# The fourth layer's experts in three passes instead of two, and a finer turn order around them

## The chip, the cores and the metric

The kernel runs on one core of a Trainium2 chip. The metric is device time in microseconds for one execution; a kernel's time is the median of several runs. TensorE is called PE here, VectorE DVE, ScalarE ACT, GpSimd POOL and SyncE SP. SP does no arithmetic in this kernel; it issues nearly all DMAs, in its program's order.

## The reference, cut to what matters

Eight layers follow each other on `x` of 8 batches of 512 rows of 128 numbers, in fp32. Each is added to `x` behind two layer norms:

```python
x = x + _layernorm(_L0_attn_ref(_layernorm(x), ...))   # softmax attention
x = x + _layernorm(_L0_ffn_ref(_layernorm(x), ...))    # token mix, gated
x = x + _layernorm(_L1_attn_ref(_layernorm(x), ...))   # a small network, trained step by step
x = x + _layernorm(_L1_ffn_ref(_layernorm(x), ...))    # 8 experts, one per row
x = x + _layernorm(_L2_attn_ref(_layernorm(x), ...))   # linear attention
x = x + _layernorm(_L2_ffn_ref(_layernorm(x), ...))    # 8 experts, each picks its rows
x = x + _layernorm(_L3_attn_ref(_layernorm(x), ...))   # softmax attention
x = x + _layernorm(_L3_ffn_ref(_layernorm(x), ...))    # 4 experts by position
```

The third layer is a scan over the 8 batches: each step computes gradients of a two-layer network (with an exact gelu, so an error function), updates its weights, and uses the new weights for its output; batch 7 has to wait for batch 6. The fourth layer sends each row to one expert, with a place counted from the first batch on, and drops rows beyond an expert's 256 places:

```python
oh = (routes[:, None] == jnp.arange(E)[None, :]).astype(jnp.int32)
pos = (jnp.cumsum(oh, axis=0) * oh).sum(-1) - 1
keep = pos < capacity
slot = jnp.where(keep, routes * capacity + pos, E * capacity)
buf = jnp.zeros((E * capacity + 1, D), x.dtype).at[slot].set(x)
h = jax.nn.relu(jnp.einsum('ecd,edh->ech', buf_e, w1) + b1[:, None, :])
y = jnp.einsum('ech,ehd->ecd', h, w2) + b2[:, None, :]
out = jnp.where(keep[:, None], y_flat[slot], x)
```

The sixth layer's experts each choose the best 512 of all 4096 rows, so it can't begin before every batch has left the fifth.

## The kernel before, in words

The program is written in the order in which Python generators are stepped, and each engine executes its instructions in that order. There are four stages.

The first stage is the first attention (`Attention.run` inside `l0`). It steps generators of the second to fourth layers between its own matmuls: `Mix.chain` (second layer), `Learn.chain` and `Learn.serve_chain` (third layer: the weight updates, and the outputs), and `Route.chain` (fourth layer: which expert and which place; it ends with four scatters, L1060, that write a batch's rows into a table by expert). These generators are still running when the attention's own work is at its end, and are handed on. Before its first load the attention calls `Route.clear` (L966), which writes zeros into the tables by expert with DMAs on SP's queue.

The second stage is called "between", and is where the change is made. An object `Rounds` holds the list of generators; `turn` steps each of them once, in the order of the list. To the generators that came from the first stage two are added:

- `Passes.chain` computes the fourth layer's experts. `PASSES = (5, B)` says that one pass serves batches 0 to 4 and another batches 5 to 7. A pass (`once`) runs all eight experts over the whole table of 8 x 256 places, whatever has been filled. It waits until its batches are routed (`while route.done < n: yield`). For an expert it loads rows (L1130), transposes them (L1136), and computes `l1f_h_ps` (L1148) with relu on ACT and DVE (L1159, L1161), then `l1f_y_ps` (L1170), adds the bias (L1172) and writes the result. Its weights, 512 KB an expert, are loaded three experts ahead. One turn holds one piece of three experts: `taken(e)`, `given(e - 2)`, `hidden(e - 1)`.
- `Pairs.chain` starts the fifth layer, one generator (`batch`) for each batch: gather the experts' results (L1265), norm, add, norm, `qkv` (L1304), linear attention, add, and the preparation of the sixth layer, whose last instruction is the store of `l2f_x` (L1406). A batch can start when its pass is done, and 5 turns after the batch ahead of it. The first one also waits for the second layer's end (`mix.over`), because the table of ACT functions is changed then. A batch has 29 steps; most are one operation on one engine, then a `yield`.

In this stage `cx.brisk` is set, so every `yield from cx.soft(...)` is no yield: the third layer's error function (L810 to L829) is one piece of DVE instructions there.

When the last batch has been routed (`while route.done < B`), the tiles of the first chains are released and `Experts` (sixth layer) loads its first weights, in the midst of the stage; `raw_b` and the transposes of L179 belong to it. The stage ends when no generator is left.

The third stage is the sixth layer, which begins with a search for each expert's threshold (from L1491 on). The fourth stage is the last attention with the last layer between its matmuls.

Tiles come from pools with a given number of buffers, in turn: `l2_o` has 3, `l2_xT` 2, the table of `qkv` tiles 4. All PSUM tiles share a ring of eight banks (`Ctx.bank`).

Of the kernel before, what the change touches and what calls it, by code (L numbers as in the profile page):

```python
# [18 lines left out]
B = 8  # L19
# [26 lines left out]

CAP1 = T // NE // 2

PASSES = (5, B)
FAR = 1 << 16  # L50


# [190 lines left out]
def free(pe=0.0, dve=0.0):  # L243

    return pe, dve, True
# [15 lines left out]
class Background:  # L261
# [19 lines left out]
    def step(self, queue, gen):  # L281
        try:
            pe, dve, is_free = costs(next(gen))
        except StopIteration:
            queue.remove(gen)
            return
        self.pe += pe
        self.dve += dve
        (self.free.add if is_free else self.free.discard)(gen)

    def turn(self, gen):

        self.first.remove(gen)
        self.first.append(gen)
        self.step(self.first, gen)
# [397 lines left out]
class Learn:  # L693
# [75 lines left out]
    def step(self, b, last):  # L769
        cx, nc = self.cx, self.cx.nc  # L770
# [39 lines left out]
        nc.vector.tensor_scalar(c, a, 0.7071067811865476, 4.0, ALU.mult, ALU.min)  # L810
        nc.vector.tensor_scalar_max(c, c, -4.0)
        nc.vector.tensor_mul(x2, c, c)
        yield from cx.soft(free(0.0, 0.9))
        nc.vector.tensor_scalar_mul(p, x2, ERF_A[0])
        for v in ERF_A[1:-1]:
            nc.vector.scalar_tensor_tensor(p, p, v, x2, ALU.add, ALU.mult)
        nc.vector.scalar_tensor_tensor(p, p, ERF_A[-1], c, ALU.add, ALU.mult)
        yield from cx.soft(free(0.0, 2.3))
        nc.vector.tensor_scalar_mul(q, x2, ERF_B[0])
        for v in ERF_B[1:-1]:  # L820
            nc.vector.scalar_tensor_tensor(q, q, v, x2, ALU.add, ALU.mult)
        nc.vector.tensor_scalar_add(q, q, ERF_B[-1])
        yield from cx.soft(free(0.0, 1.4))
        nc.vector.reciprocal(q, q)
        yield from cx.soft(free(0.0, 1.7))
        nc.vector.tensor_mul(p, p, q)
        phi, h = tile_of("phi"), tile_of("h", 2)
        nc.vector.tensor_scalar(phi, p, 0.5, 0.5, ALU.mult, ALU.add)
# [106 lines left out]
class Route:  # L935
# [5 lines left out]
    def __init__(self, cx: Ctx, w_switch, b_switch):  # L941
# [8 lines left out]
            cx.dram.tile([NE * CAP1, D], F32, name=f"l1f_{name}{i}", tag=f"l1f_{name}{i}")  # L950
            for i in range(len(PASSES))
        ]
# [24 lines left out]
    def turn(self, b):  # L977
        return sum(b >= n for n in PASSES)

# [102 lines left out]
class Passes:  # L1082
# [14 lines left out]
    def weights(self, n):  # L1097

        cx, nc, e = self.cx, self.cx.nc, n % NE
        if n >= len(PASSES) * NE:  # L1100
            return
# [18 lines left out]
    def once(self, base, rows, results):  # L1120
        cx, nc = self.cx, self.cx.nc
        NF = self.NF
        cap, ns = CAP1, CAP1 // P
        of_expert = lambda t, e: t[e * cap : (e + 1) * cap, :].rearrange("(s p) d -> p s d", p=P)
        loads, xts, hts = {}, {}, {}

        def load(e):
            if e < NE:
                loads[e] = cx.work([P, ns, D], "l1f_xg", bufs=4)
                nc.sync.dma_start(loads[e], of_expert(rows, e))  # L1130

        def taken(e):
            xg = loads.pop(e)
            t = cx.bank("l1f_xT_ps")
            for s in range(ns):
                nc.tensor.transpose(t[:, s * P : (s + 1) * P], xg[:, s, :], cx.ident)  # L1136
            xts[e] = cx.work([D, cap], "l1f_xT")
            nc.vector.tensor_copy(xts[e], t[:, :cap])
            load(e + 4)

        def hidden(e):
            hts[e] = cx.work([P, NF, cap], "l1f_hT")
            xt = xts.pop(e)
            for f2 in range(NF // 2):
                hp = cx.bank("l1f_h_ps")
                for i in range(2):
                    f = 2 * f2 + i
                    nc.tensor.matmul(  # L1148
                        hp[:, i * cap : (i + 1) * cap],
                        self.ws[base + e][0][:, f * P : (f + 1) * P],  # L1150
                        xt,
                        start=True,
                        stop=True,
                    )
                for i in range(2):
                    f = 2 * f2 + i
                    src, bias = hp[:, i * cap : (i + 1) * cap], self.b1c[:, f, e : e + 1]
                    if i == 0:
                        nc.scalar.activation(hts[e][:, f, :], src, AF.Relu, bias=bias)  # L1159
                    else:  # L1160
                        nc.vector.tensor_scalar(hts[e][:, f, :], src, bias, 0.0, ALU.add, ALU.max)  # L1161

        def given(e):
            ht = hts.pop(e)
            w2 = self.ws.pop(base + e)[1]
            yp = cx.bank("l1f_y_ps")
            for s in range(ns):
                ss = slice(s * P, (s + 1) * P)
                for f in range(NF):
                    nc.tensor.matmul(yp[:, ss], ht[:, f, ss], w2[:, f, :], start=(f == 0), stop=(f == NF - 1))  # L1170
            y = cx.work([P, ns, D], "l1f_y")
            nc.vector.tensor_add(  # L1172
                y,
                yp[:, :cap].rearrange("p (s d) -> p s d", d=D),
                self.b2b[:, e * D : (e + 1) * D].unsqueeze(1).to_broadcast([P, ns, D]),
            )
            nc.sync.dma_start(of_expert(results, e), y)
            self.weights(base + e + 3)

        for e in range(4):  # L1180
            load(e)
        yield
        for e in range(NE + 2):
            if e < NE:
                taken(e)
            if e >= 2:
                given(e - 2)
            if 1 <= e <= NE:
                hidden(e - 1)
            yield  # L1190


class Rounds:


    def __init__(self, chains):
        self.chains = list(chains)

    def add(self, chain):
        self.chains.append(chain)  # L1200

    def turn(self):
        for chain in list(self.chains):
            try:
                next(chain)
            except StopIteration:
                self.chains.remove(chain)


class Pairs:  # L1210
# [23 lines left out]
    def chain(self, passes, mix, rounds):  # L1234

        cx = self.cx
        for _ in range(3):
            yield
        self.w, self.gw = (
            cx.transposed(w, n, raw=raw) for w, n, raw in zip(self.args, ("w2a", "w2f_gate"), self.raws)  # L1240
        )
        while not mix.over:
            yield
        cx.nc.scalar.preload_act_table_set("natural_log_exp_and_others")
        for b in range(B):
            while passes.done <= self.route.turn(b):
                yield
            rounds.add(self.batch(b))
            for _ in range(5 if b + 1 < B else 0):
                yield  # L1250

    def batch(self, b):
        cx, nc, route = self.cx, self.cx.nc, self.route
# [696 lines left out]
@with_exitstack  # L1950
def kernel(ctx: ExitStack, tc: tile.TileContext, a: dict, out: bass.AP):
    cx = Ctx(ctx, tc, a["consts"])
    nc = tc.nc
    for b in range(B):
        nc.sync.dma_start(cx.x[b], a["L0_attn_x"][b].rearrange("(j p) d -> p j d", p=P))
    of = lambda layer, *names: [a[f"{layer}_{n}"] for n in names]
    route = Route(cx, *of("L1_ffn", "w_switch", "b_switch"))
    right = ExitStack()
    with cx.phase("first"):
        cx.w = right.enter_context(tc.tile_pool(name="chains", bufs=2, side="right"))  # L1960
        with cx.beside("attention") as ca:
            mix = Mix(cx, *of("L0_ffn", "W_r", "W_k", "W_v", "mu_r", "mu_k"))
            learn = Learn(cx, route, *of("L1_attn", "t_k", "t_v", "t_q", "W1", "b1", "W2", "b2"))
            chains = l0(cx, Attention(ca), *of("L0_attn", "Wq", "Wk", "Wv"), mix, learn)

        cx.brisk = True
        with cx.beside("between") as cb:
            rounds = Rounds(chains)
            passes = Passes(cb, route, *of("L1_ffn", "w1", "b1", "w2", "b2"))
            pairs = Pairs(cb, route, *of("L2_attn", "W_qkv"), *of("L2_ffn", "gate_w"))  # L1970
            rounds.add(passes.chain())
            rounds.add(pairs.chain(passes, mix, rounds))
            while route.done < B:
                rounds.turn()
            right.close()
            ce = right.enter_context(cx.beside("experts", side="right"))
            experts = Experts(ce, pairs, *of("L2_ffn", "ln_w", "ln_b", "fc1s", "b1s", "fc2s", "b2s"))
            while rounds.chains:
                rounds.turn()
    cx.brisk = False  # L1980
    with cx.phase("last"):
        at = Attention(cx)
        ffn = L3Ffn(cx, *of("L3_ffn", "W1", "b1", "W2", "b2", "Wu", "bu"), out)
        with cx.beside("staging") as cs:
            cs.home = cx.home
            weights = l3_weights(cs, *of("L3_attn", "Wqkv", "bqkv", "Wout", "bout"))
            ffn.load()
            weights = experts.run(cs, weights)
        right.close()
        cx.w = right.enter_context(tc.tile_pool(name="tiles", bufs=2, side="right"))  # L1990
        with right:
            l3(cx, at, experts, ffn, weights)
# [62 lines left out]
```

## Time and profile before

| | us |
|---|---|
| median of 3 runs | 2139.75 |
| the runs | 2133.82 to 2141.98 |
| the profiled execution, its own time | 2144.43 |
| its span, from first to last instruction | 2142.6 |

| engine | busy us | share of the span |
|---|---|---|
| PE (matmuls) | 1772.7 | 83% |
| PEld (weight loads) | 1019.4 | 48% |
| DVE | 1265.6 | 59% |
| ACT | 1084.8 | 51% |
| POOL | 502.9 | 23% |

One row of a view is one instruction or a group of them: start, duration, engine, line in the kernel, operation, what it writes and reads, and in brackets how long the engine was idle before it and what ended that. PEclk is the share of full speed that TensorE's clock was granted. The busy share of an engine is an average over stages; what a stage is bound by is read from its own rows.

### The profile page before, as it was taken

To read this page: it belongs to the slowest core of one execution; us is meant where nothing else is said; L and a number is where in the kernel's file an instruction comes from. 1 tells how busy PE (TensorE), PEld (TensorE's weight loads), DVE (VectorE), ACT (ScalarE), POOL (GpSimd) and SP (SyncE) were. 2 spreads that over 40 slices of the span, in tenths; PEclk is the share of its full clock that TensorE was granted. 3 is DMA by queue.
4 is the path that set the end of the run, shared out by engine and by line. 5 is a ranking of instruction groups with operands and counts; after the bars stand their busy time and mean duration, and the time that the engine had idled before them with its cause. 6 is when DMAs were issued, how large, how long until landed. Compare 5 with 4: busy or idle time off the path is not lost.

```text
span 2142.6 us, 31783 instructions
## 1 busy us (share of the span) xinstructions
PE 1772.7 (83%) x10918; PEld 1019.4 (48%) x10918; DVE 1265.6 (59%) x3840; ACT 1084.8 (51%) x2272; POOL 502.9 (23%) x574
## 2 busy tenths in 40 slices
PE   3999899999989757467646773899999999999998
PEld 1444445454444446446336552444444445454566
DVE  2677776868676455446547322776666666566322
ACT  1566655656545433246651221366666565656553
POOL 1001110212111130453523484222122121110010
PEclk7899999899889868579565786799999999999999
DMA  5212101111010103134323132111101011000000
GB/s 126 36 36 37 31 20 29 27 32 38 15 26 11 54 21 96 44 92 113 87 75 99 25 43 34 32 31 29 28 7 32 9 31 29 12 7 11 1 11 11
DMA packets 197920, 81.84 MB, mean 38 GB/s; under 512 B 97460, under 2 KB 189530, under 8 KB 197760
## 3 DMA queue, kind: packets, MB, share of 16 engines
q1 hardware_dynamic: 190080, 73.61, 14.3%
q0 software_dynamic: 7680, 6.19, 1.9%
q8 instruction: 88, 1.44, 0.3%
q14 instruction: 72, 0.59, 0.1%
HBM read 45.25 MB, written 31.59 MB: 36 GB/s over the span
## 4 chain that ended last, share of the span: by engine, by line
PE 59%; DVE 23%; issue 5%; POOL 5%; ACT 4%; DMA 2%; SPq 1%; POOLq 0%; ACTq 0%; DVEq 0%
PE at_s L402 13%; PE at_o L420 11%; DVE at_mx L403 8%; PE at_st L409 7%; PE l3f_y_ps L1923 5%; PE l3f_h_ps L1916 5%; DVE ln_st L203 3%; PE flip L239 3%; POOL l2f_out L1679 2%; POOL l2f_xg L1074 1%; POOL ln_rs L194 1%; PE l2a_qkv_ps L1304 1%; PE l1f_h_ps L1148 1%; PE l1f_y_ps L1170 1%; PE at_ops L434 1%
## 5 line engine op out<-in xcount | busy, mean ns | idle before, releaser
L403 DVE TENSOR_REDUCE at_mx<-at_s 128x1 f32<-128x512 f32 x1024 | 639.5, 681 | 281.4 <-PE at_st L409 217.8
L412 ACT ACTIVATE at_e<-at_st 128x512 f32<-128x512 f32 x1024 | 533.8, 597 | 214.0 <-PE at_st L409 189.3
L402 PE MATMUL at_s<-qk 32*128 32x512 f32 x2048 | 585.7, 652 | 28.1 <-DMA qk<-qk_zero 21.1
L409 PE MATMUL at_st<-qk 32*128 32x512 f32 x2048 | 567.3, 656 | 9.4 <-ACT at_e L412 4.6
L402 PEld LDWEIGHTS at_s<-qk 32*128 32x128 f32 x2048 | 221.4, 194 | 179.2 <-issue 74.0
L194 POOL TENSOR_TENSOR ln_rs<-ln_ve,mhalf 128x4 f32<-128x4 f32 x136 | 138.6, 1019 | 700.9 <-DVE ln_ve L188 607.3
L409 PEld LDWEIGHTS at_st<-qk 32*128 32x128 f32 x2048 | 218.4, 191 | 107.0 <-issue 41.5
L420 PE MATMUL at_o<-at_e,pad_v 128*32 128x512 f32 x2048 | 246.8, 625 | 9.9 <-DVE at_mx L403 9.8
L420 PEld LDWEIGHTS at_o<-at_e,pad_v 128*32 128x32 f32 x2048 | 63.5, 114 | 190.2 <-issue 156.9
L1923 PEld LDWEIGHTS l3f_y_ps<-w3f,l3f_hT 128*128 128x128 f32 x1024 | 129.3, 193 | 41.9 <-issue 30.9
L1923 PE MATMUL l3f_y_ps<-w3f,l3f_hT 128*128 128x128 f32 x1024 | 133.0, 277 | 0.6 <-ACT l3f_hT L1917 0.5
L1916 PE MATMUL l3f_h_ps<-l3f_xT,w3f 128*128 128x512 f32 x256 | 130.8, 606 | 0.1
L1917 ACT ACTIVATE l3f_hT<-l3f_h_ps,w3f_b1c 128x512 f32<-128x512 f32 x128 | 87.3, 689 | 84.0 <-PE l3f_h_ps L1916 83.8
L428 ACT COPY at_ot<-at_o 128x512 f32<-128x512 f32 x64 | 37.5, 586 | 173.8 <-PE at_o L420 173.8
L1926 DVE SCALAR_TENSOR_TENSOR l3f_o<-l3f_y_ps,l3f_w,l3f_o 128x128 f32<-128x128 f32 x128 | 44.5, 349 | 117.7 <-PE l3f_y_ps L1923 117.4
L217 ACT ACTIVATE l_xn<-x,ln_off,ln_rs 128x128 f32<-128x128 f32 x96 | 39.4, 482 | 72.4 <-DVE ln_off L211 72.3
L239 PE MATMUL flip<-consts_sb,l_xn 128*128 128x128 f32 x96 | 30.8, 411 | 47.8 <-ACT l_xn L217 47.6
L375 POOL COPY pad_v<-l_in 128x128 f32<-128x128 f32 x32 | 9.4, 293 | 246.2 <-DMA l_in<-l_v 216.0
L203 DVE BATCH_NORM_STATS2 ln_st<-x 128x6 f32<-128x128 f32 x256 | 55.2, 278 | 9.6 <-POOL x L1366 3.3
L1766 POOL TENSOR_TENSOR l_qk<-l_r,consts_sb 128x256 f32<-128x256 f32 x32 | 22.0, 687 | 159.0 <-DVE l_r L1761 159.0
L434 PE MATMUL at_ops<-consts_sb,at_ot 128*128 128x128 f32 x256 | 42.2, 288 | 18.1 <-DVE at_mx L403 16.6
L1679 POOL DMA_INDIRECT l2f_out<-l2f_y,l2f_idx x32 | 50.7, 1585 | 25.4 <-DVE l2f_y L1676 16.6
(388 smaller groups left out, 2514.7 us busy)
## 6 DMA issues: line engine op xcount, KB each, us to landing
l1f_w<-in_L_ffn_w SPq DMA_DIRECT2D x32, 256.0 KB
l2f_parts<-l2f_out SPq DMA_DIRECT2D x32, 256.0 KB
l2f_out<-l1f_zero SPq DMA_DIRECT2D x24, 256.0 KB
l_qk<-l_qkT SPq DMA_DIRECT2D x16, 256.0 KB
qk<-l_qk SPq DMA_DIRECT2D x128, 32.0 KB
qk<-at_mt SPq DMA_DIRECT2D x256, 2.0 KB
qk<-l_qkT SPq DMA_DIRECT2D x128, 32.0 KB
l2f_x<-l2f_rows SPq DMA_DIRECT2D x8, 272.0 KB
```

What stands on the lines that cost most here:

```text
L194: self.nc.gpsimd.tensor_tensor(rs, ve, self.mhalf[:, :NJ], ALU.pow)
L203: nc.vector.bn_stats(st[:, j, :], src[:, j, :])
L239: self.nc.tensor.transpose(t[:, j * P : (j + 1) * P], src[:, j, :], self.ident)
L402: nc.tensor.matmul(s, qk[:, 0, c * P : (c + 1) * P], qk[:, 1, :], start=True, stop=True)
L403: nc.vector.tensor_reduce(mx[n][:, c, h : h + 1], s, AX.X, ALU.max, negate=True)
L409: nc.tensor.matmul(s, qk[:, 1, c * P : (c + 1) * P], qk[:, 0, :], start=True, stop=True)
L412: nc.scalar.activation(es[g][:, h, :], s, AF.Exp, scale=scale)
L420: nc.tensor.matmul(o[32 * h : 32 * h + 32, :], vp[:, c, h, :], e[:, h, :], start=(c == 0), stop=(c == NJ - 1),)
L1679: nc.gpsimd.indirect_dma_start(out=self.pairs.summed[s], out_offset=bass.IndirectOffsetOnAxis(ap=idx[e][:, s : s + 1], axis=0), in_=ys[e][ ...
L1916: nc.tensor.matmul(hp, self.w1[:, e, f * P : (f + 1) * P], xt, start=True, stop=True)
L1917: nc.scalar.activation(hts[e][:, f], hp, AF.Relu, bias=self.b1c[:, f, e : e + 1])
L1923: nc.tensor.matmul(yp[:, :D], hts[e][:, f, js], self.w2[:, e, f, :], start=(f == 0), stop=(f == NF - 1))
```

## The change

Six edits, all for the second stage:

1. `PASSES` becomes `(4, 6, B)`: three passes, for batches 0 to 3, 4 and 5, 6 and 7. There is a third pair of tables by expert (`taken`, `given`), so `clear` writes 24 pieces of zeros instead of 16.
2. In the third layer four yields around the error function are unconditional, so they hold in the second stage too.
3. A pass has two turns for an expert: `taken` and `given` in one, `hidden` in the other.
4. `Rounds` has two lists. `first` holds the first stage's chains and the passes' chain; the fifth layer's chains are in `chains`. In a turn `first` is stepped once for every two of `chains`, between them.
5. A batch of the fifth layer follows the one ahead by 4 turns, or by 2 for batches 6 and 7, instead of by 5.
6. The loops' ends ask both lists.

```diff
-PASSES = (5, B)
+PASSES = (4, 6, B)
...
-        yield from cx.soft(free(0.0, 0.9))
+        yield free(0.0, 0.9)
         nc.vector.tensor_scalar_mul(p, x2, ERF_A[0])
...
-        yield from cx.soft(free(0.0, 2.3))
+        yield free(0.0, 2.3)
         nc.vector.tensor_scalar_mul(q, x2, ERF_B[0])
...
-        yield from cx.soft(free(0.0, 1.4))
+        yield free(0.0, 1.4)
         nc.vector.reciprocal(q, q)
-        yield from cx.soft(free(0.0, 1.7))
+        yield free(0.0, 1.7)
         nc.vector.tensor_mul(p, p, q)
...
             if e >= 2:
                 given(e - 2)
+            yield
             if 1 <= e <= NE:
                 hidden(e - 1)
-            yield
+                yield
...
 class Rounds:
-    def __init__(self, chains):
-        self.chains = list(chains)
+    def __init__(self, first):
+        self.first = list(first)
+        self.chains = []
 
     def add(self, chain):
         self.chains.append(chain)
 
-    def turn(self):
-        for chain in list(self.chains):
+    def step(self, queue):
+        for chain in list(queue):
             try:
                 next(chain)
             except StopIteration:
-                self.chains.remove(chain)
+                (self.first if chain in self.first else self.chains).remove(chain)
+
+    def turn(self):
+        rest = list(self.chains)
+        for i in range(0, max(len(rest), 1), 2):
+            self.step(self.first)
+            self.step(rest[i : i + 2])
+
+    @property
+    def over(self):
+        return not self.first and not self.chains
...
             rounds.add(self.batch(b))
-            for _ in range(5 if b + 1 < B else 0):
-                yield
+            if b + 1 < B:
+                for _ in range(4 if b < PASSES[-2] - 1 else 2):
+                    yield
...
-            rounds = Rounds(chains)
             passes = Passes(cb, route, *of("L1_ffn", "w1", "b1", "w2", "b2"))
             pairs = Pairs(cb, route, *of("L2_attn", "W_qkv"), *of("L2_ffn", "gate_w"))
-            rounds.add(passes.chain())
+            rounds = Rounds([*chains, passes.chain()])
             rounds.add(pairs.chain(passes, mix, rounds))
...
-            while rounds.chains:
+            while not rounds.over:
                 rounds.turn()
```

## The prediction

> **What bounds the kernel now.** The change touches one of four stages, so I first found that stage. In the page's slices (53.6 us each) the stage between the two attentions is slices 14 to 21: PE loses its nines there and its clock falls to 5 or 6 tenths.
>
> ```profile
> PE   3999899999989757467646773899999999999998
> ...
> PEclk7899999899889868579565786799999999999999
> ```
>
> In the timeline it runs from 738 us (last write of the first attention) to 1125 us (first step of the fifth layer's search): 387 us. I cut it where one phase ends and another begins, and asked for busy time by stretch (columns: length, PE, PEld, DVE, ACT, POOL busy with counts, granted clock, DMA share, GB/s):
>
> ```profile
> 738.00:801.00 63.00, 33.03 (x169) 27.63 (x167) 32.48 (x132) 16.46 (x39) 17.16 (x21) 0.62 0.18 53
> 801.00:828.00 27.00, 26.71 (x183) 24.01 (x182) 14.82 (x56) 12.89 (x30) 5.60 (x5) 1.00 0.43 122
> 828.00:866.00 38.00, 25.15 (x156) 22.90 (x157) 17.72 (x54) 6.13 (x16) 2.01 (x2) 0.78 0.27 80
> 866.00:948.00 82.00, 34.25 (x123) 24.85 (x122) 35.38 (x183) 28.70 (x65) 43.50 (x41) 0.59 0.12 33
> 948.00:1000.00 52.00, 46.74 (x296) 41.35 (x296) 34.50 (x154) 30.65 (x68) 17.32 (x16) 0.95 0.52 152
> 1000.00:1125.00 125.00, 69.70 (x234) 45.45 (x234) 64.43 (x348) 75.59 (x169) 50.39 (x48) 0.63 0.30 83
> 738.00:1125.00 387.00, 235.58 (x1157) 186.18 (x1155) 199.34 (x923) 170.43 (x385) 135.98 (x132) 0.70 0.28 79
> ```
>
> No engine is full over the stage (PE 61%, DVE 52%). Only 948 to 1000, the second expert pass, is full (PE 90%). Elsewhere latency rules: one chain's ACT, PE, DVE and POOL in turn. The waits by pair and the timeline show the crudest case, the mixing layer's error function, about 9 us of DVE in one piece while PE's queue is stuck behind its result:
>
> ```profile
> PE l1a_hT_ps L835 <- DVE l1a_h L829: 30.1, 3, 11.0
> ...
> 825.88 1.89 PE L1148 MATMUL l1f_h_ps<-l1f_xT,l1f_w 128*128 128x256 f32 x8
> 837.97 1.01 PE L835 MATMUL l1a_hT_ps<-consts_sb,l1a_h 128*32 128x128 f32 x4 [10.19 <-DVE l1a_h L829]
> ```
>
> The last 125 us are linear-attention chains alone. The stores of `l2f_x` (the last DMA of batches 4 to 7) date their ends:
>
> ```profile
> 1063.35 0.36 SPq L1406 DMA_DIRECT2D l2f_x<-l2f_rows  x1
> ...
> 1097.41 0.36 SPq L1406 DMA_DIRECT2D l2f_x<-l2f_rows  x1
> ...
> 1111.25 0.36 SPq L1406 DMA_DIRECT2D l2f_x<-l2f_rows  x1
> ...
> 1123.01 0.36 SPq L1406 DMA_DIRECT2D l2f_x<-l2f_rows  x1
> ```
>
> Read with the code's turns: 11 turns with three batches alive between the first two (34.06 us, 3.10 a turn), then 5 turns with two (2.77), then 5 with one (2.35). The five turns with four before that took 17.5 us (3.50). So a turn costs about 2.0 us + 0.36 us for each live batch. Putting more batches into fewer turns pays.
>
> **The change, part by part.** I counted turns from the generators: a batch's chain has 29 steps, 232 in all; the stage has 94 turns now.
>
> *A third pass.* It adds eight experts. Their price is that of the second pass, from the groups of 948 to 1000:
>
> ```profile
> L1170 PE MATMUL l1f_y_ps<-l1f_w,l1f_hT 128*128 128x128 f32 x128 | 16.6, 279 | 1.7 <-DVE l1f_hT L1161 1.5 <-ACT l1f_hT L1159 0.2
> L1148 PE MATMUL l1f_h_ps<-l1f_xT,l1f_w 128*128 128x256 f32 x64 | 15.1, 379 | 0.0
> ...
> L1136 PE MATMUL l1f_xT_ps<-consts_sb,l1f_xg 128*128 128x128 f32 x16 | 3.5, 307 | 0.0
> ```
>
> That is 35.2 us of PE, 4.4 an expert, and half of the stage's pass rows elsewhere: 14 us DVE, 7 us ACT; plus 32 DMAs (row loads, weights, results; 6 MB), which the 0.52 DMA share of that stretch carries. *Rule against row:* the Trainium skill, "TensorE: Matmul & The Clock Gate", Part 1, says the array falls to half clock after about 3.4 us without work. Passes spread into a half-idle stage could then cost twice, 70 us. But the first pass, interleaved with other chains, ran at a granted 1.00 and the second at 0.95, so I take 35; 70 stays for the upper end.
>
> *Clearing the third table.* `clear` issues 24 DMAs instead of 16, on SP's queue, ahead of the first attention's loads:
>
> ```profile
> 26.09 9.01 SPq L966 DMA_DIRECT2D l1f_taken<-l1f_zero  x16
> ...
> 35.14 1.92 SPq L535 DMA_DIRECT2D l_in<-l_v  x4
> ...
> 40.70 5.73 PE L402 MATMUL at_s<-qk 32*128 32x512 f32 x24 [15.71 <-DMA qk<-qk_zero]
> ```
>
> PE waits for exactly this queue. *Rule against row:* "DMA: Bandwidth & Descriptors", Anatomy of one DMA, gives about 50 ns of sequencer dispatch; eight would be 0.4 us. The row says 9.01/16 = 0.563 us each. The row decides: 8 x 0.563 = **+4.5 us**, at a place with no cover.
>
> *First pass over batches 0 to 3.* It no longer waits for batch 4's routing, so it starts at turn 5 instead of 14, with two turns an expert, and ends at turn 23 instead of 24. Its PE work falls into the stretch 738 to 801, where PE is at half load. The unconditional yields split the error function (9 us) over five turns, so a pass half-step stands between its pieces. Turns 1 to 10 stay at 38 us; 11 to 15 hold the 11.6 us of DVE of today's turn 11, five half-steps at 0.85 us and the other mixing layer's 2.5 (18.5 us); 16 to 20 hold five half-steps (11 us PE) and the learning step's 12 us PE (23 us); 21 to 23 about 10 us. End: 738 + 89.5 = 828. Today at 828 the learning of batch 7 stands at the same place, but the pass ends only at 861. The split yields cost the learning chain four more turns a batch; what covers them is the pass's PE work, and with that gone each batch would pay 4 x 2.4 us (the tail's lone-chain turn).
>
> *Two batches to a turn of the first chains.* From turn 28 each turn has 2, later 3 or more, sub-turns. From 828 to the last batch routed there are 28 sub-turns. Batch 7's learning needs 10 of them: 15 us for five with its first matmul and the error function's DVE, 17 for the five PE steps behind it (3.4 each), so 860 (now 866). The next 18 hold learning's end, two routings and nearly the whole second pass, with PE 35 + 22 us (the 34.25 of 866 to 948 less 50 batch steps at 0.25, which is the second pass's 46.7 - 35.2 over its 47 steps); at 3.6 us, between the 3.1 of three live chains and the 4.1 of 866 to 948 (20 turns), that is 65 us, and 10 us for the stall at the end that exists today (PE idle 939 to 948.7, behind row loads, which wait for the scatter, and `raw_b`). Last batch routed and picked up: 935, against 948.
>
> The third pass then takes 20 sub-turns, each half an expert and 1.7 batch steps. PE: 35.2 + 34 steps x 0.25 = 44 us at the 90% load of today's second pass: 49 us, ending at 984, with batches 0 to 5 in flight.
>
> *The tail.* It has 32 turns with 166 steps (now 40 turns with 133: the formula gives 128 for a measured 125). 32 x 2.0 + 166 x 0.36 = 124 us. The gain sits here: staggering by 4, then 2 turns puts up to 8 batches into a turn. `l2_o` has 3 buffers; batch 7's first load must wait about two turns for batch 5's, on SP, with batch 0's stores queued behind it and POOL's gather waiting after it; I put that at 1 us, inside the rounding. The last three batches' stores (1.3 MB each) come two turns apart instead of five; at 122 GB/s the share was 0.43, so the engines carry about 284 GB/s, 4.6 us a batch, and two turns are about 5 us: just enough.
>
> **Sum.** 984 + 124 + 4.5 = 1112.5 against 1125: -12.5 us. The first attention and everything after 1125 keep their instruction order. The profiled execution's own time, 2144.4, becomes 2132. It lies 4.7 above the median of the runs, 2139.75, which becomes **2127 us**, -0.6%. About 0.5% (10.7 us) is what a measurement of this kernel can tell from no change.
>
> **The rivals.**
>
> *Slower: the crowded tail.* The 0.36 us was read at one to four batches and is used at eight. All engines queue in order; if steps get in each other's way, the slope grows. Even point: (1125 - 4.5 - 984 - 64) / 166 = 0.44 us a step. ACT alone was busy 75.6/133 = 0.57 us a step; if the slope goes there, the tail is 158 us, the stage ends 22 us later than today: about 2161. For it: eight steps a turn are 4.5 us of ACT, nearly the 4.9 us the formula gives. Against: up to 4.6 batches a turn no bend is seen (3.45 and 3.78 us).
>
> *No change: the sub-turns are dear.* If the 28 sub-turns cost 4.15 us as the turns of 866 to 948 do, routing ends at 944, the pass at 993, the tail at 1117; with 4.5 that is -3.5 us: 2136. For it: PE's queue holds pass, learning and batch in one order, so a pass that waits for a scatter (one start more than now) stops the learning chain too.
>
> *More gain: the clock.* The stage's 0.70 could rise towards 0.95 with passes from turn 5 to 44; `qkv` matmuls take 2.92 us for four in the tail and 1.29 inside the second pass. 1.6 us less for each of eight batches and as much again in other matmuls: 2127 - 25 = 2102.
>
> That the change doesn't do what it says is excluded: the new instruction order holds 112 more matmuls (8 x 14), no other new work on PE, and the turns given above.
>
> **How the numbers follow.** Forecast 0.40, clock 0.10, no change 0.27, crowded tail 0.23. Half-widths of about 10 us around each case spread the forecast over both sides of -0.5%: faster by over 0.5%: 0.48; within: 0.29; slower: 0.23. The range leaves out the last tenth on each side: 2104 to 2158. The likeliest case alone: 2115 to 2139.
>
> **What would show it.** Right: the first L402 matmul about 4.5 us later; `l1f_h_ps` from about 765 on; the third wait of L835 covered by L1148 and L1170; last scatter (L1060) near 930; the last pass's L1170 ending near 988; last `l2f_x` store near 1110; tail turns of 4.5 to 5 us at eight batches. Wrong: tail turns over 5.5 us (crowding), a last scatter after 945 (dear sub-turns), a clock above 0.8 over the stage with a store before 1100 (clock).

## The result, and the profile after

The changed kernel takes a median of 2167.9 us (four runs, 2157 to 2172) against 2140.9 for the kernel before: a ratio of 1.0118, 95% interval 1.0092 to 1.0144. A second comparison of the same two kernels gave 1.0084 (1.0057 to 1.0112). It is slower by about 1%, where 0.6% faster was forecast.

To compare many traces I use one measure below, the **stage**: from the start of the last `at_rec` (L437, the end of the first attention) to the last store of `l2f_x`. Before it is 1123.01 - 736.66 = 386.4 us. After, the timeline has its start on DVE:

```profile
746.89 0.26 DVE L437 RECIPROCAL at_rec<-at_ops 128x16 f32<-128x16 f32 x1 [5.05 <-PE at_ops L434]
```

and on SP's queue its end, the last batch's store:

```profile
1149.14 0.36 SPq L1420 DMA_DIRECT2D l2f_x<-l2f_rows  x1
```

1149.14 - 746.89 = 402.3 us, +15.9. The measure is steady: a second profile of the changed kernel gives 402.0, and the three two-pass variants e1, g1 and g2 below give 383.8, 383.9 and 383.9. It shows one or two us that the runs' times, which scatter over 10 to 25 us, don't.

The page's slices (54.2 us each) of after show PE fuller in the stage (slices 14 to 21 or so) and the clock a little higher:

```profile
PE   2999899999989766768656783799999999999998
...
PEclk7899999898989877679675686799999999999999
```

Busy time by stretch, cut at the same points of the program as before (stage start; end of turn 23, where the learning step of batch 7 begins and the first pass now ends; learning of batch 7 done; last batch routed and picked up; last pass ended; end). Columns: length, PE, PEld, DVE, ACT, POOL busy with counts, clock, DMA share, GB/s:

```profile
748.00:849.00 101.00, 74.20 (x418) 63.82 (x416) 49.68 (x185) 31.66 (x71) 21.33 (x25) 0.78 0.29 85
849.00:888.00 39.00, 23.80 (x99) 20.18 (x99) 17.69 (x70) 6.19 (x17) 12.89 (x13) 0.52 0.22 64
888.00:973.00 85.00, 58.41 (x304) 48.53 (x302) 39.57 (x179) 26.91 (x64) 30.08 (x29) 0.80 0.30 85
973.00:1021.00 48.00, 43.64 (x252) 36.94 (x252) 24.23 (x85) 19.87 (x41) 10.33 (x10) 0.89 0.51 148
1021.00:1150.00 129.00, 77.23 (x298) 55.08 (x298) 83.31 (x438) 93.97 (x212) 60.74 (x57) 0.71 0.31 89
```

Before, these stretches are 90, 38, 83, 48 and 128 us, with the end of the first pass in the second of them. None became shorter. The last pass takes as long for two batches as it took for three, since a pass goes through all rows of its table, filled or not. Most of the loss, 11 of 15 us, lies in the first stretch, 101 us instead of 90, with PE busy 74 us instead of 60.

The waits by pair over the stage (waited in all, times, longest), first before, then after, say what happened there (the pass and the error function, in 738 to 1150 us of both traces):

```profile
PE l1a_hT_ps L835 <- DVE l1a_h L829: 30.1, 3, 11.0
ACT l1a_hT L837 <- PE l1a_hT_ps L835: 26.6, 3, 10.7
ACT l1f_hT L1159 <- PE l1f_h_ps L1148: 20.9, 19, 3.2
DVE l1f_hT L1161 <- ACT l1f_hT L1159: 20.8, 20, 3.1
```

```profile
ACT l1f_hT L1159 <- PE l1f_h_ps L1148: 58.5, 38, 13.6
DVE l1f_hT L1161 <- ACT l1f_hT L1159: 38.5, 33, 6.2
ACT l1a_hT L837 <- PE l1a_hT_ps L835: 18.2, 3, 8.7
PE l1a_hT_ps L835 <- DVE l1a_h L829: 5.7, 2, 3.1
```

The wait that the split yields aimed at, L835 for the error function, went from 30.1 to 5.7 us (3.0 more of it now ends on another releaser, `l1f_eq`). In its place ACT waits 58.5 us for the pass's matmuls and DVE 38.5 us for ACT's half of the hidden layer. One such wait, in order of time:

```profile
796.10 0.75 DVE L663 SCALAR_TENSOR_TENSOR l0f_mix<-l0f_xT,mu,l0f_mix 128x512 f32<-128x512 f32 x1
...
796.99 2.04 PE L668 MATMUL l0f_k_ps<-l0f_mix,w0f 128*128 128x512 f32 x2 [3.96 <-DVE l0f_mix L663]
798.83 1.91 PE L676 MATMUL l0f_r_ps<-w0f,l0f_mix 128*128 128x128 f32 x8
...
800.54 2.91 PE L1148 MATMUL l1f_h_ps<-l1f_xT,l1f_w 128*128 128x256 f32 x8
...
802.49 0.47 ACT L1159 ACTIVATE l1f_hT<-l1f_h_ps,w1f_b 128x256 f32<-128x256 f32 x1 [1.11 <-PE l1f_h_ps L1148]
803.00 0.48 DVE L1161 TENSOR_SCALAR l1f_hT<-l1f_h_ps,w1f_b 128x256 f32<-128x256 f32 x1 [6.15 <-ACT l1f_hT L1159]
...
804.39 0.28 DVE L814 TENSOR_SCALAR l1a_p<-l1a_x 128x256 f32<-128x256 f32 x1
```

L814, the next piece of the error function, has had its input since L812 ended at 794.5 us. It stands in DVE's queue behind L1161, the pass's eviction (the copy of a matmul's result out of PSUM), which waits for ACT, which waits for PE's L1148, which stands behind another chain's matmuls (L668, L676). DVE is idle for 6.15 us with work behind it. ACT's own piece is 0.5 us of that; the rest is the wait for PE.

The start of the span: SP clears three tables, and the first matmul is 3.8 us later (44.52 against 40.70).

```profile
25.71 13.20 SPq L966 DMA_DIRECT2D l1f_taken<-l1f_zero  x24
```

At the end of the attention's first step 1.3 us of it are left (the first `at_rec` at 90.66 us against 89.41), and none in a second profile of the changed kernel (87.95). The stage's start is 10.2 us late (746.89 against 736.66): 7.3 us of this appear in one place, between 490 and 536 us, where the instructions are the same. The busy time by stretch of the changed kernel in its first profile, then in its second:

```profile
496.00:512.00 16.00, 16.00 (x73) 11.30 (x72) 8.88 (x34) 6.90 (x16) 0.56 (x1) 0.50 0.10 26
```

```profile
496.00:512.00 16.00, 15.65 (x113) 7.42 (x105) 14.91 (x50) 9.95 (x23) 2.46 (x3) 0.89 0.21 45
```

In the first, PE was busy without a gap and had a clock of 0.50 for 16 us: 73 matmuls instead of 113. In the second profile the stage starts at 735.23. So this part is the execution's, not the change's. What the change itself costs by the traces is 15.9 us of stage and up to 3.8 us of clearing: 16 to 20 us, 0.7 to 0.9%. The second ratio agrees with that; the first lies above it, and its interval begins where that ends.

### The profile page after: what moved, and what is told of

The parts are those of the page before. It is cut to its first block, busy times and chain, and to the rows that moved or that the text cites. A ratio compares the mean times of both kernels' runs of the same rounds, so it can differ in the third digit from the quotient of the medians.

```text
span 2169.6 us, 32337 instructions
## 1 busy us (share of the span) xinstructions
PE 1825.5 (84%) x11126; PEld 1062.7 (49%) x11126; DVE 1280.7 (59%) x3872; ACT 1093.3 (50%) x2288; POOL 502.2 (23%) x574
## 3 DMA queue, kind: packets, MB, share of 16 engines
q1 hardware_dynamic: 201984, 80.96, 15.2%
## 4 chain that ended last, share of the span: by engine, by line
PE 33%; DVE 10%; issue 4%; POOL 3%; ACT 3%; DMA 1%; SPq 0%; POOLq 0%; ACTq 0%; DVEq 0%
PE at_s L402 6%; PE at_o L420 5%; PE l3f_y_ps L1937 5%; PE l3f_h_ps L1930 5%; DVE at_mx L403 4%; PE at_st L409 4%; PE flip L239 2%; POOL l2f_out L1693 2%; DVE ln_st L203 1%; POOL l2f_xg L1074 1%; PE l1f_y_ps L1170 1%; PE l_qkv_ps L1773 1%; PE l1f_h_ps L1148 1%; DVE l2f_junk L1513 1%; DVE l_u L1782 1%
## 5 line engine op out<-in xcount | busy, mean ns | idle before, releaser
L402 PE MATMUL at_s<-qk 32*128 32x512 f32 x2048 | 588.5, 653 | 32.5 <-DMA qk<-qk_zero 25.2
L402 PEld LDWEIGHTS at_s<-qk 32*128 32x128 f32 x2048 | 221.3, 194 | 183.2 <-issue 76.2
L1148 PE MATMUL l1f_h_ps<-l1f_xT,l1f_w 128*128 128x256 f32 x192 | 58.0, 456 | 4.9 <-DVE l1f_xT L1138 4.9
L1170 PE MATMUL l1f_y_ps<-l1f_w,l1f_hT 128*128 128x128 f32 x384 | 56.3, 300 | 6.2 <-DVE l1f_hT L1161 4.7
L434 PE MATMUL at_ops<-consts_sb,at_ot 128*128 128x128 f32 x256 | 41.8, 286 | 18.1 <-DVE at_mx L403 16.6
```

The lines of the kernel that those rows point to most:

```text
L402: nc.tensor.matmul(s, qk[:, 0, c * P : (c + 1) * P], qk[:, 1, :], start=True, stop=True)
L1148: nc.tensor.matmul(hp[:, i * cap : (i + 1) * cap], self.ws[base + e][0][:, f * P : (f + 1) * P], xt, start=True, stop=True,)
```

## The experiments

Each gives its ratio to the kernel before and its stage. "Old turns" means the kernel before as base, "new turns" the changed one.

**e1: new turns, two passes.** The stagger stays at 4 turns, and 2 behind batches 5 and 6.

```
-PASSES = (4, 6, B)
+PASSES = (5, B)
...
-                for _ in range(4 if b < PASSES[-2] - 1 else 2):
+                for _ in range(4 if b < 5 else 2):
```

> The changed kernel with two passes, over batches 0 to 4 and 5 to 7, instead of three; turn order, split error function and stagger of 4, then 2, stay. Theory "the pass": the third pass is what costs (35 us of PE that can't all be hidden, 4 us of clearing), the turn order itself is harmless or helps: about 2135 to 2145. Rival "the turn order": the finer turns with a pass step and a learning step in each are what lengthened the stage, and the third pass is hidden as forecast: about 2160 to 2170, like the changed kernel (2168).

Measured: 0.9982 (0.9968 to 0.9996), stage 383.8: the pass, not the turn order.

**e2: old turns, three passes.** `PASSES = (4, 6, B)` in the kernel before.

> The kernel before with three passes, over batches 0 to 3, 4 and 5, 6 and 7, and nothing else of the change. "The pass": slower than before by about what the change costs, 2160 to 2175. "The turn order": 2130 to 2145, the time before with 4 us of clearing and the earlier start of the batches' chains.

Measured: 1.0168 (1.0142 to 1.0194), stage 420.0. So a third pass costs 33.6 us of stage in the old turns, about its 35.2 us of PE, and 402.3 - 383.8 = 18.5 us in the new ones. With three passes the new turns take 420.0 - 402.3 = 17.7 us off, with two passes 2.6: the turn order helps, but not enough.

**e3: the learning's yields soft again.**

```
-        yield free(0.0, 0.9)
+        yield from cx.soft(free(0.0, 0.9))
```

(and the three others)

> The changed kernel with the four yields inside the mixing layer's error function soft again (no turn given there in this stage), so that its 9 us of DVE stand in one piece. "The pass": within 6 us of the changed kernel, 2162 to 2174. "The turn order": these four added turns a batch are part of what lengthened the routing, each about 2.4 us or more for three batches; without them 2145 to 2158.

Measured: 1.0106 (1.0078 to 1.0134), stage 408.0. The four added yields a batch are no loss; they save 5.7 us of stage.

**e4: old turns, two passes, new stagger.**

```
-            for _ in range(5 if b + 1 < B else 0):
-                yield
+            if b + 1 < B:
+                for _ in range(4 if b < 6 else 2):
+                    yield
```

> The kernel before with the batches' chains started 4 turns apart, the last 2, instead of 5; two passes and old turns stay. The stage has 88 turns instead of 94. By the formula for a turn (2.0 us and 0.36 us for each live batch) six turns less are 12 us: 2128. If a turn's cost lies in its batch steps and not in the turn (as the changed kernel's tail, 129 us for fewer turns, may say), it stays at 2137 to 2142.

Measured: 0.9985 (0.9968 to 1.0002), stage 385.4, 1.0 us less. The program has 90 turns, four fewer than the kernel before and not the six of the expectation; by the formula four are 8 us. Turns are not what the tail is paid in here; the last pass ends 12.4 us later, and the end is the same.

**f1: the clearing alone.** A third table `l1f_spare` in the kernel before, only cleared.

```
-        for taken in self.taken:
+        for taken in (*self.taken, self.spare):
```

> The kernel before with a third table, which nothing uses, cleared with the two (24 DMAs on SP's queue ahead of the first attention's loads instead of 16). As forecast (8 x 0.563 us with no cover): 4 to 5 us over before, 2146 to 2148. Rival (the delay is taken up inside the first attention, as the shift of +1 to +3 us at 90 to 490 us in the changed kernel's trace says): 0 to 2 us over before.

Measured: 1.0024 (1.0001 to 1.0047), +5.1 us by the ratio, stage 386.4 as before. The timeline has the eight issues, and behind them the first matmul:

```profile
35.14 4.25 SPq L967 DMA_DIRECT2D l1f_spare<-l1f_zero  x8
```

```profile
45.01 4.03 PE L402 MATMUL at_s<-qk 32*128 32x512 f32 x16 [19.94 <-DMA qk<-qk_zero]
```

4.3 us later than before (40.70). The interval, 0.2 to 10.1 us, reaches down to nearly nothing: the forecast's size fits, and so does the rival's, that the attention takes part of the delay up again. The first `at_rec` is 2.2 us later than before (91.62).

**f2: half of one pass left out.** In pass k, experts 4 to 7 give PE, ACT and DVE nothing to do.

```
+        full = NE // 2 if base == k * NE else NE
...
+            if e >= full:
+                return load(e + 4)
...
         def hidden(e):
+            if e >= full:
+                return
```

> The changed kernel with the PE, ACT and DVE work of experts 4 to 7 left out of the first pass (their DMAs and all turns stay; zeros are stored as their results). Four experts are 17.6 us of PE. "Half-idle" (the forecast: the first pass falls into a stretch where PE is at half load and costs nothing): 0 to 3 us under the changed kernel, 2164 to 2168. "Round trips" (every engine's queue is in order, so a pass step's trip from PE to ACT to DVE stands in front of the chains' work, wherever the pass lies): 10 to 18 us under it, 2150 to 2158.

Measured: 1.0068 (1.0049 to 1.0087), stage 398.6: 3.7 us less for 17.6 us of PE.

> The same for the second pass (batches 4 and 5). "Half-idle": it lies among learning and routing, where the forecast's 3.6 us a sub-turn were set by chains: 2 to 6 us under the changed kernel, 2162 to 2166. "Round trips": 10 to 18 us under it, 2150 to 2158.

Measured: 1.0063 (1.0039 to 1.0088), stage 399.0: 3.3 us less.

> The same for the third pass (batches 6 and 7), which both theories hold to be bound by PE (91% busy in its 47 us): 15 to 20 us under the changed kernel, 2148 to 2153. If it were less than 10, the pass would be bound by the batches' chains beside it and not by PE.

Measured: 1.0010 (0.9991 to 1.0030), stage 391.1: 11.2 us less, between the two marks of the expectation, so PE bounds the third pass only in part. The ratios, against the first 1.0118, would have said 11, 12 and 23 us and pointed to "round trips" everywhere; the stages, which don't carry the rest of the execution, say that the later halves of the first two passes are mostly hidden.

**f4: the changed kernel again.**

> The changed kernel as it is, beside the others of this call. The stages of the traces (stage +14 to +16 us, clearing +4 to +5) add up to a ratio of 1.008 to 1.010; the first comparison said 1.0118 from four runs. 1.008 to 1.010: clearing and stage are the whole of it. 1.012 or more: some 5 us are lost outside the stage and still to be named.

Measured: 1.0084 (1.0057 to 1.0112), stage 402.0. No loss outside the stage and the clearing is needed to explain it.

**f3: the other half of the first pass left out,** `if e < none` in place of `if e >= full`, with none = 4 for the first pass.

> The changed kernel with the PE, ACT and DVE work of experts 0 to 3 left out of the first pass (DMAs and turns stay, zeros are stored as their results): the half that stands among the chains that wait for one another (767 to 824 us, PE clock 0.71), where leaving out experts 4 to 7 took away the half at full clock and shortened the stage by 4 us. "Paid in the chains' gaps": PE work placed between chains that wait for each other lengthens them by nearly all of its time, so the stage is 8 to 18 us shorter and the turns 6 to 15 take about 38 us instead of 57: ratio 1.000 to 1.005. "Half-idle": as for the other half, 2 to 4 us: ratio 1.006 to 1.008.

Measured: 1.0036 (1.0019 to 1.0052), stage 385.2: 17.1 us less, all that these four experts take of PE, where the other four of the same pass took 3.7. The loss has a place: turns 5 to 14, in which these experts lie.

**g1: two passes, clearing behind the fourth load of the first attention.**

```
-                learn.route.clear()
...
+        if n == 3:
+            learn.route.clear()
```

> Two passes with the new turns (ratio 0.998) and the 16 clearing DMAs issued behind the first attention's fourth load instead of ahead of its first. If the clearing has no cover where it stands (8 DMAs more cost 4.4 us at the first L402 matmul), 16 moved away give 8 to 9 us: first L402 at about 31 us, ratio 0.994. If something else holds the first matmul there (the projections' own loads), 0 to 3 us: 0.997 to 0.998.

Measured: 0.9995 (0.9979 to 1.0010), stage 383.9. Neither: the first L402 is at 33.80 instead of 39.95 (e1), 6.2 us earlier, but nothing of it is left at the first `at_rec` (89.24 against 88.05 in e1). The moved clearing now stands in SP's queue ahead of a later step's loads, and PE waits there:

```profile
62.25 8.46 SPq L967 DMA_DIRECT2D l1f_taken<-l1f_zero  x16
...
76.31 2.11 PE L409 MATMUL at_st<-qk 32*128 32x512 f32 x8 [6.72 <-DMA qk<-at_mt]
```

The stage's start (742.17 against 735.28) is later still. Part of that is the clock: its loss in the first attention, taken as PE's busy time x (1 - granted clock) and summed over 2 us, is 54 us here and 45 in e1, and lies between 36 and 61 us over all profiles.

**g2: g1 with the hidden tile split** in one for ACT and one for DVE.

```
-            hts[e] = cx.work([P, NF, cap], "l1f_hT")
+            hts[e] = cx.work([P, NF // 2, cap], "l1f_hT"), cx.work([P, NF // 2, cap], "l1f_hU")
```

> The kernel of the run before this one with the pass's hidden tile split in two, one written by ACT and one by DVE, so that DVE's eviction doesn't wait for ACT's (14.2 us of such waits in 764 to 826 us of the changed kernel). If the pass's steps cost what their trip from PE over ACT to DVE takes, 0.95 us less for each of two pieces and 16 experts of two passes, a third to all of it in sight: 5 to 20 us less, ratio 0.985 to 0.992. If PE's own time is what is paid, no change to the kernel before it: within 3 us.

Measured: 1.0001 (0.9983 to 1.0020), stage 383.9: no change. With two passes the first one starts behind turn 13, so this wasn't the place to ask; k3 asks again, and shows that the split leaves DVE's wait for ACT as it is.

**h0: f3 with PE's part put back.** For experts 0 to 3 the transposes and matmuls are issued at their turns on the weights, and nothing reads them.

```
+            if e < none:
+                w1 = self.ws[base + e][0]
...
+                        nc.tensor.matmul(
+                            hp[:, i * cap : (i + 1) * cap], w1[:, f * P : (f + 1) * P], w1[:, :cap], start=True, stop=True
+                        )
+                return
```

> The kernel without experts 0 to 3 in the first pass (stage 384 us against 400 to 401 with them), with PE's part of them put back: the same number of transposes and matmuls at the same turns, on the weights as data, with no ACT or DVE work behind them (their results stay zeros). "PE time": what stands in PE's queue ahead of the chains' matmuls is what is paid: stage 395 to 402. "Trips": PE's gaps do hide it, and what is paid is the wait of ACT and DVE for the pass's pieces ahead of the chains' own: stage 384 to 390.

Measured: 1.0012 (0.9993 to 1.0030), stage 385.3 against 385.2 without any of it. PE's time is hidden, all of it, where PE needn't wait for the pass's copies on DVE and ACT. The same place as above in h0's timeline:

```profile
787.93 0.42 DVE L812 TENSOR_TENSOR l1a_x<-l1a_c 128x256 f32<-128x256 f32 x1
...
790.88 0.29 DVE L814 TENSOR_SCALAR l1a_p<-l1a_x 128x256 f32<-128x256 f32 x1
791.11 1.10 PE L668 MATMUL l0f_k_ps<-l0f_mix,w0f 128*128 128x512 f32 x2 [1.85 <-DVE l0f_mix L663]
...
792.04 1.05 PE L676 MATMUL l0f_r_ps<-w0f,l0f_mix 128*128 128x128 f32 x8
...
792.93 1.89 PE L1151 MATMUL l1f_h_ps<-l1f_w 128*128 128x256 f32 x8
```

PE has the same L1151 (L1148 there) between the chains, but L814 runs as soon as DVE's own work lets it. The busy time of the first 101 us, first without the experts (f3), then with their PE part (h0):

```profile
746.00:847.00 101.00, 59.94 (x333) 51.26 (x330) 53.81 (x209) 30.72 (x71) 24.99 (x28) 0.70 0.33 100
```

```profile
748.00:849.00 101.00, 71.84 (x440) 63.28 (x438) 53.81 (x209) 30.90 (x71) 25.26 (x28) 0.80 0.34 100
```

107 more matmuls, 12 us more of busy PE, the same DVE work done, and a clock of 0.80 instead of 0.70: the fuller PE also ran faster, so "hidden" is a net of both.

**h1: first pass held** until batch 4 is routed, three passes.

```
-            while route.done < n:
+            while route.done < max(n, 5):
```

> The changed kernel, three passes, but the first pass (still over batches 0 to 3) waits until batch 4 is routed too, so that it starts behind the turns 6 to 13 instead of in them. "Place": experts cost 17 us for four in those turns and 4 for four behind them, so the stage goes from 401 to 386 to 392. "The third pass": the work is only put off, and the passes behind it start later by as much: 397 to 402.

Measured: 1.0080 (1.0050 to 1.0110), stage 401.7. "Place" fails as a cure: the last pass ends 10.2 us earlier (262.2 us into the stage against 272.4), and the tail behind it is 9.6 us longer. The first four batches' chains start with the end of the first pass, now later, so more of their steps should be left to the tail; that is argued, not measured apart.

**h2: two passes split at six,** `PASSES = (6, B)` in e1.

> Two passes with the new turns, over batches 0 to 5 and 6 and 7, instead of 0 to 4 and 5 to 7. For a gain: only two batches instead of three are left to the tail behind the second pass, 29 steps x 0.36 = 10 us. Against: the batches' chains start a routing later, at the end of a first pass that starts about 30 us later, so fewer steps are done beside the second pass. If the second pass and routing set the end: stage 372 to 380 (382 split at 5). If the start of the chains sets it: 384 to 400.

Measured: 1.0046 (1.0028 to 1.0064), stage 394.3. The start of the chains decides, not how few batches are left.

**k1: the hidden layer evicted by ACT alone,** three passes.

```
-                    if i == 0:
-                        nc.scalar.activation(hts[e][:, f, :], src, AF.Relu, bias=bias)
-                    else:
-                        nc.vector.tensor_scalar(hts[e][:, f, :], src, bias, 0.0, ALU.add, ALU.max)
+                    nc.scalar.activation(hts[e][:, f, :], src, AF.Relu, bias=bias)
```

> The changed kernel with the pass's hidden layer evicted by ACT alone (four pieces an expert on ACT instead of two on ACT and two on DVE). "DVE at the head": in 764 to 826 us DVE stood 14.2 us behind ACT's pieces with the error function queued after it; without those pieces the stage goes from 401 to 384 to 394 us. "Any trip": ACT's two more pieces (0.47 us each) lengthen the trip to the result by as much as DVE's wait, and the learning chain needs ACT too: 398 to 404.

Measured: 1.0067 (1.0052 to 1.0082), stage 395.3, 7.0 less. In its timeline:

```profile
790.97 0.42 DVE L812 TENSOR_TENSOR l1a_x<-l1a_c 128x256 f32<-128x256 f32 x1
...
793.68 0.28 DVE L814 TENSOR_SCALAR l1a_p<-l1a_x 128x256 f32<-128x256 f32 x1
...
801.40 0.69 DVE L685 SCALAR_TENSOR_TENSOR l0f_t<-l0f_r,l0f_v_ps 128x512 f32<-128x512 f32 x1 [4.68 <-PE l0f_v_ps L683]
```

L814 no longer stands behind the pass, but the next head of DVE's queue does: L685 waits 4.68 us for L683, which PE takes only behind the pass's L1148.

**k3: three passes, hidden tile split** as in g2.

> The changed kernel, three passes, with the hidden tile split in two so that DVE's piece needs not wait for ACT's. If DVE's wait for ACT is what is paid, the stage goes from 401 to 388 to 396; if DVE then waits as long for PE's matmul, 398 to 402, as the two-pass version's 382.4 against 382.1 suggests.

Measured: 1.0083 (1.0065 to 1.0102), stage 402.4. No change, but the edit doesn't do what it was meant to: with tiles of their own, DVE's piece still waits for ACT's. In k3's timeline ACT's L1159 ends at 790.95 us, and then:

```profile
790.98 0.48 DVE L1161 TENSOR_SCALAR l1f_hU<-l1f_h_ps,w1f_b 128x256 f32<-128x256 f32 x1 [6.15 <-ACT l1f_hT L1159]
```

The waits of this pair over the stage are 38.0 us (38.5 in the changed kernel). So neither g2 nor k3 tells what DVE's wait for ACT costs beside the wait for the matmul. The timeline above does for one piece: 0.5 of 6.15 us.

**k2: two passes and the hidden layer on ACT.**

> Two passes over batches 0 to 4 and 5 to 7 with the new turns (stage 382), the hidden layer evicted by ACT alone. "DVE at the head": the first pass starts behind the error function here, so less is to be had: 374 to 381. "Any trip": 382 to 386.

Measured: 0.9962 (0.9951 to 0.9974), stage 377.7, 6.1 less than e1: 2139.2 us beside 2147.5 for the kernel before in the same comparison. "DVE at the head", as expected, and the fastest version here: 0.4% under the kernel before. That is within the 0.5% named in the prediction, but the interval of this comparison leaves no change out.

## Why the prediction was wrong, point by point

The forecast had -17 us of stage (without the clearing); it was +15.9. By its own steps:

| step | forecast | measured |
|---|---|---|
| clearing | +4.5 | +3.8 at the first matmul, 0 to 1.3 left at 90 us; +5.1 (0.2 to 10.1) alone |
| turns 1 to 10 | 38 | 45 |
| turns 11 to 15 | 18.5 | 29.8 |
| turns 16 to 20 | 23 | 18 |
| turns 21 to 23 | 10 | 8 |
| turn 24 to last batch routed | 107 | 124 |
| third pass | 49 | 46 to 48 |
| tail | 124 | 128 to 130 |

(Turns were found in the trace by counting each engine's instructions in the program's order; up to turn 23 one ends with its last instruction on DVE, and turn 1 begins where the forecast's 738 us lies, 1.3 us into the stage.)

The stage is 33 us longer than forecast: about 19 in turns 1 to 15, 17 between turn 24 and the last batch routed, 4 to 6 in the tail, and 7 less in turns 16 to 23.

**The step that failed: "Its PE work falls into the stretch 738 to 801, where PE is at half load",** with the pass put at nothing in turns 1 to 10 and turns 11 to 15 summed from DVE's durations and half-steps. PE's half load does hide the pass's PE work: h0 shows all of it hidden. But the pass isn't PE work alone. Each half-step leaves a piece on ACT and DVE that waits for PE, and in a queue that runs in order the pieces of other chains behind it wait as well. In turns 11 to 15 DVE is busy 17.9 us, nearly the 18.5 of the sum; what the sum had at nothing is the 11.9 us that DVE stands idle between. The same turns by kernel, in us:

| turns | changed | k3, split tile | k1, ACT only | f3, without experts 0 to 3 | h0, their PE part only | e1, two passes |
|---|---|---|---|---|---|---|
| 1 to 10 | 45 | 45 | 45 | 37 | 39 | 37 |
| 11 to 15 | 29.8 | 29.8 | 21.4 | 21.4 | 19.4 | 18.5 |
| 16 to 20 | 18 | 18 | 21 | 18 | 18 | 22 |
| 21 to 23 | 8 | 8 | 8 | 8 | 8 | 10 |

The forecast's 18.5 for turns 11 to 15 is what e1, with only two copies of the pass in them, takes. From the stage's start to the end of turn 15 the changed kernel takes 76.4 us and h0 59.8. Of these 16.6 us, DVE's own added work is 6.8 (busy 40.0 against 33.2), and DVE standing idle is 9.8 (36.4 against 26.6): the waiting is more of the loss than the work. From the start of L812 to the end of L829, the error function with what stands between its pieces takes 23.7 us in the changed kernel and in k3, 19.4 in k1, and 15.2 in h0. Of the 17 us that experts 0 to 3 cost, moving DVE's piece of the hidden layer to ACT gives back at most 7.0 (k1, which changes the other passes too); the other 10 were not taken apart further (the copies of `l1f_xT`, the sums of `l1f_y`, and PE's own waits on them).

**Turn 24 to the last batch routed: 107 forecast, 124 measured.** The ten sub-turns to the end of batch 7's learning took 39 us where 32 were summed, and the next eighteen 76 (888 to 964 us), 4.2 each: not the forecast's 3.6 but the 4.15 of the rival "the sub-turns are dear". The stall at the end is there as forecast (964 to 973.5, with 10 taken). The rival's mark, a last scatter after 945, shows it: the scatter is at 968.98 (958.8 on the time axis of before, whose stage starts 10.2 us earlier).

```profile
968.98 0.98 POOL L1060 DMA_INDIRECT l1f_taken<-l1f_xn,l1f_place  x1 [2.94 <-issue]
```

So that rival's price was right, and its sum (-8 us of stage) still wrong, because it took turns 1 to 23 from the forecast. Half of the second pass, which lies there, costs 3.3 us (f2), so a whole one some 7 if both halves are alike; the other 10 us over the forecast weren't taken apart.

**Right:** the clearing by the row (4.5) as the time on SP's queue: f1 measured 4.25 us for eight issues. The 50 ns of dispatch that the Trainium skill gives ("DMA: Bandwidth & Descriptors", Anatomy of one DMA), of which eight would be 0.4, stand there for DMAs issued from GpSimd, which these are not. That the place has "no cover" is not shown: of the 3.8 us, 1.3 or less are left at 90 us. The third pass's price, by the groups of the stretch it fills (17.5 + 16.9 + 3.7 = 38 us of PE where 35.2 were taken):

```profile
L1170 PE MATMUL l1f_y_ps<-l1f_w,l1f_hT 128*128 128x128 f32 x128 | 17.5, 283 | 0.1
L1148 PE MATMUL l1f_h_ps<-l1f_xT,l1f_w 128*128 128x256 f32 x64 | 16.9, 411 | 0.0
...
L1136 PE MATMUL l1f_xT_ps<-consts_sb,l1f_xg 128*128 128x128 f32 x16 | 3.7, 316 | 9.4 <-DMA l1f_xg<-l1f_taken 9.4
```

**The tail** came out by its formula within 5 us, so the *crowded tail*, the rival on the slower side, is not the cause: its even point was 0.44 us a step, and (129 - 64)/166 gives 0.39. But the gain that the formula promised for fewer turns never appeared. Before, the tail is 127 us with 40 turns, now 130 with 32 and more steps: level, as forecast. What should have paid was an earlier end of the passes, and they end later (1019.3 - 746.9 = 272.4 us into the stage; 259.5 before). e4 shows the trade: four turns less, and 1.0 us gained.

**The clock** did rise, from 0.70 to 0.75 over the stage, and did not pay. That the matmuls which it speeds up are not those that the chains wait for is argued, not measured. The Trainium skill's rule of half clock after idle ("TensorE: Matmul & The Clock Gate", Part 1) was set aside in the forecast because passes ran at 0.95 to 1.00. Between the chains of turns 6 to 15 they didn't: the L1148 above took 2.91 us, 1.89 in h0.

## What to carry to other kernels

Work is hidden in a half-idle stretch only if all of its pieces are. Here filling PE's gaps cost nothing, but each eviction that the work leaves at the head of another engine's in-order queue held up the chains behind it. So price interleaved work in three parts: the time on the engine with room, the time that its pieces take on the engines that the other chains wait for (6.8 us of DVE here), and the time that those engines stand idle at the head of their queues (9.8 us). Moving evictions to an engine with fewer chains behind it gave back 6 to 7 us (k1, k2). A batched step whose cost doesn't fall with the batch (here a pass over a table of fixed size) shouldn't be cut finer unless the added piece is known to be hidden.

## What the runs showed of the hardware that I had not expected

The clock of a full PE can fall to half. In the stretch 496 to 512 us above, PE was busy 16.00 of 16 us and got 0.50; the second profile of the same program got 0.89 there. Over the twenty profiles here the first attention (first L402 to the stage's start) took 683 to 708 us. Less the loss to the clock, worked out as in g1 (36 to 61 us), it is 645 to 654. A difference of 10 us between two single profiles of this kernel, or between medians of four runs, says little; the stage's own length, repeated within 0.3 us, says much.

A short stall can cost PE twice. After 3.96 us idle, L668, L676 and L1148 took 2.04 + 1.91 + 2.91 us; after 1.85 us, in h0, 1.10 + 1.05 + 1.89. That is 2.8 us on top of the stall, and the granted clock accounts for it: 0.50 from 797 to 801 us in the changed kernel, 1.00 from 791 to 795 us in h0. The clock's stretches at 0.50 in this stage last 3.4 us or whole multiples of it (6.8 us here), the length that "TensorE: Matmul & The Clock Gate", Part 1, of the Trainium skill gives for its window. But the clock fell 2.7 us into the stall and not after 3.4, and in the stretch above it fell with PE busy, so "no stall of 3.4 us" is not enough to keep it up here.
